# Wd of every expert kept on chip and addressed by a register, in a mixture-of-experts layer whose weights come by gather

## The chip, the cores and the metric

The kernel runs on one core of a Trainium2 chip. The metric is the device time of one execution in microseconds; where several executions were made, the median is given. The engines are named as the profile names them: PE (matrix multiply, with PEld for its weight loads), DVE (vector), ACT (scalar), POOL (the general engine, which here also issues the indirect DMAs) and SP (which issues the plain DMAs). All data are 32-bit floats.

## The reference, cut to what matters

Eight sequences of 256 tokens with 128 features pass through four blocks, each with a layer norm in front and a residual behind: a gated delta-net attention of 16 heads, a small feed-forward with the signs of a weight matrix, a causal softmax attention (16 query heads in 4 groups), and a mixture of experts. The change touches only the last. What it computes, for a token `x` and its normalised form `n`:

```python
s = softmax(n @ Wr.T)                    # 8 experts
s1, s2, e1, e2 = top2(s)                 # two largest and their experts
y = 0
for s_i, e in ((s1, e1), (s2, e2)):
    h = relu(n @ Wg[e].T) * (n @ Wu[e].T)    # 512 hidden features
    y += s_i / (s1 + s2 + eps) * (h @ Wd[e].T)
out = x + y
```

Each expert has three matrices of 512 x 128 (`Wg`, `Wu`) and 128 x 512 (`Wd`), 262 KB each; all eight experts' `Wd` are 2.1 MB.

## The kernel before, in words

The kernel has two stages. The first, up to about 883 us of the span, is the gated delta-net attention; its result `xr` is stored to DRAM (`x1`) sequence by sequence at line 953. The second stage opens new pools at line 995, loads `x1` back into eight tiles `x0` to `x7` (line 1003) and the weights of the later blocks (lines 1005 to 1019) with SP, and does the other three blocks.

Nothing in the second stage is scheduled by the compiler's order. Each part of the work is a Python generator that yields `Unit`s: the engine, an estimated duration, what it needs, which buffers it takes and gives back, what it sets, and how much later a DMA's data land (`lands`). The function `merge` plans all generators against each other on this estimate and emits the instructions in the planned order. An engine executes its instructions in this order, and waits on semaphores for what comes from other engines.

The experts work on token lists. Sequences 0 to 5 form one segment (12 token tiles of 128) and sequences 6 and 7 a second (4 token tiles). For each segment `lists_of` makes, on DVE and PE, a list of slots sorted by expert, padded so that every slot tile of 128 rows belongs to one expert: 31 slot tiles for the first segment and 15 for the second, 46 in all. It leaves `seg.tok` (which token stands in each slot), `seg.at` (where a token's two slots are) and `seg.ex`. In the kernel before, `seg.ex` (the tile `exi`) holds for slot tile k, in partition p, the row number 128 x expert + p.

Then for every slot tile k:

- `fetched()` (line 1463, POOL) gathers `we`, the tile of weights of the slot tile's expert, by an indirect DMA of 128 rows of 6144 bytes (786 KB): per partition 512 elements each of `Wg`, `Wu` and `Wd`. There are 7 such buffers (`WE`).
- `gathered()` (line 1451, POOL) gathers `xs`, the 128 normalised token rows (64 KB), into one of 8 buffers.
- `turned_rows()` (line 1474, PE) transposes them, and `taken_rows()` (line 1480, ACT) copies the result to SBUF as `xsT`.
- `hidden()` (line 1489, PE) makes 8 matmuls of 128 x 128 x 128 into the PSUM tile `gu`: four for `Wg`, four for `Wu`. There are two such PSUM tiles.
- `gated()` has ACT take the relu of the first half (line 1495) and DVE multiply it with the second (line 1497), which gives `h`.
- `projected_hidden()` (line 1504, PE) makes 4 accumulating matmuls with the `Wd` part of `we`, which gives `o`, and gives the buffer of `we` back.
- `stored()` copies `o` to `y` (line 1516, DVE) and stores it to DRAM (SP).

On PE the steady order is `o` of tile k, the transpose of tile k+4, `gu` of tile k+2. At the end `results()` gathers each token's two rows back (POOL) and `combined()` adds them, weighted, into `x` (line 1540, DVE) and stores the output.

A matmul in the profile is written `out<-stationary,moving`; the multiplication in 32-bit floats shows as two records for each `mm` call, so `gu` has 16 per tile and `o` 8.

Of the kernel before, what the change touches and what calls it, by code (L numbers as in the profile page):

```python
# [10 lines left out]
F32 = mybir.dt.float32  # L11
I32 = mybir.dt.int32
# [6 lines left out]
P = 128  # L19
B, T, D = 8, 256, 128  # L20
# [9 lines left out]
E, DFF = 8, 512  # L30
NF = DFF // P
# [4 lines left out]
WE = 7  # L36
# [110 lines left out]
def block_kernel(ctx: ExitStack, tc: tile.TileContext, a, out):  # L147
    nc = tc.nc
# [85 lines left out]
    wp = gx.enter_context(tc.tile_pool(name="g_w", bufs=1))  # L234
# [9 lines left out]
    with tc.tile_pool(name="g_ln", bufs=2) as lp, tc.tile_pool(name="g_lp", bufs=4, space=PSUM) as pp:  # L244
        x = lp.tile([P, NT, D], F32, name="x", bufs=1)
# [4 lines left out]
        for q in range(4):  # L250
# [3 lines left out]
            ps = pp.tile([P, 4, P], F32, tag="ps", name=f"lnpsa{q}")  # L254
# [5 lines left out]
        ps = pp.tile([P, NBC, 2 * NPR], F32, tag="ps", name="gateps")  # L260
# [33 lines left out]
        for lhsT, dst, name in ((le, pin, "pin"), (gt, dec, "dec"), (cross, pend, "pend")):  # L294
            ps = pp.tile(shape, F32, tag="ps", name=f"{name}ps")
# [3 lines left out]
    with (  # L299
# [36 lines left out]
        class Seq:  # L336


            def __init__(self):
                self.w, self.wv, self.sq = [], [], {}  # L340
                self.kq, self.vt, self.S = [None] * NH, {}, [None] * NH
                self.dm, self.pbs, self.at, self.g, self.gp = {}, {}, {}, {}, {}
                self.kk, self.ws, self.o, self.taken, self.oT, self.osq = {}, {}, {}, {}, {}, {}
                self.kb, self.kd, self.yn = {}, {}, {}
# [650 lines left out]
    with (  # L995
# [21 lines left out]
        nc.sync.dma_start(rank, a["rank"])  # L1017
        lc = wp.tile([P, N_LISTS], F32, name="lc")
        nc.sync.dma_start(lc, a["lists"])

        sgn = wp.tile([P, D], F32, name="sgn")
        neg = wp.tile([P, D], F32, name="neg")
# [39 lines left out]
        at = [Attended() for _ in range(B)]  # L1062
# [209 lines left out]
        class Tokens:  # L1272


            def __init__(self, t0, n):
                self.t0, self.n, self.s = t0, n, t0
                self.kt = (2 * n * P + E * (P - 1)) // P
                self.xn = dram.tile([n * P, D], F32, name=f"xn{t0}")
                self.ys = dram.tile([self.kt * P, D], F32, name=f"ys{t0}")
                self.lg = wp.tile([P, n, E], F32, name=f"lg{t0}")  # L1280
                self.xs, self.xsT, self.ps, self.h, self.o, self.y, self.we = {}, {}, {}, {}, {}, {}, {}

        segs, t0 = [], 0
        for n in LISTS:
# [17 lines left out]
        def lists_of(seg):  # L1302


            s, n, kt = seg.s, seg.n, seg.kt

            def tmp(name, shape, dtype=F32):
                return wp.tile([P] + shape, dtype, name=f"l_{name}{s}")
# [41 lines left out]
            ps = pp.tile([P, n + 1, E], F32, tag="ps", name=f"place{s}")  # L1350
# [50 lines left out]
            ex = tmp("ex", [kt])  # L1401
            nc.vector.tensor_reduce(ex, past, AX.X, ALU.add)
            nc.vector.tensor_scalar(ex, ex, float(E - 1), None, ALU.min)

            nc.vector.tensor_scalar(ex, ex, float(P), lc[:, L_ID : L_ID + 1], ALU.mult, ALU.add)
            seg.ex = tmp("exi", [kt], I32)
            nc.vector.tensor_copy(seg.ex, ex)
            yield Unit("DVE", 0.05, sets=(("experts", s),))

            intile = tmp("intile", [2, n, kt])  # L1410
# [9 lines left out]
            for c0 in range(0, 2 * n, step):  # L1420
# [6 lines left out]
                if c0 == 0:  # L1427
                    ps = pp.tile([P, kt], F32, tag="ps", name=f"token{s}")
# [29 lines left out]
        def fetched():  # L1458

            for seg, k in every:  # L1460
                yield Unit("POOL", 1.25, needs=(("experts", seg.s),), take=("we",), sets=(("we", seg.s, k),), lands=5.0)
                seg.we[k] = sp.tile([P, 3, NF, P], F32, tag="we", name=f"we{seg.s}_{k}", bufs=WE)
                nc.gpsimd.indirect_dma_start(
                    out=seg.we[k].rearrange("p a f c -> p (a f c)"),
                    out_offset=None,
                    in_=a["we"],
                    in_offset=bass.IndirectOffsetOnAxis(ap=seg.ex[:, k : k + 1], axis=0),
                )

        def turned_rows():  # L1470
# [11 lines left out]
        def hidden():  # L1482

            for seg, k in every:
                yield Unit("PE", 1.75, needs=(("x", seg.s, k, 0), ("we", seg.s, k)), take=("p2",), give=("xsT",), sets=(("gu", seg.s, k),), late=0.3)
                seg.ps[k] = p2.tile([P, 2, NF, P], F32, tag="p2", name=f"gu{seg.s}_{k}")
                for i in range(2):
                    for f in range(NF):
                        mm(seg.ps[k][:, i, f], seg.we[k][:, i, f], seg.xsT[k], start=True, stop=True)  # L1489
# [8 lines left out]

        def projected_hidden():
            for seg, k in every:  # L1500
                yield Unit("PE", 0.88, needs=(("h", seg.s, k),), take=("ps",), give=("h", "we"), sets=(("o", seg.s, k),), late=0.2)
                seg.o[k] = pp.tile([P, D], F32, tag="ps", name=f"o{seg.s}_{k}")
                for f in range(NF):
                    mm(  # L1504
                        seg.o[k],
                        seg.h[k][:, f],
                        seg.we[k][:, 2, f],
                        start=(f == 0),
                        stop=(f == NF - 1),
                    )  # L1510
# [34 lines left out]
        with tc.manual_schedule():  # L1545
            merge(
                [
                    turned_rows(),
                    taken_rows(),
                    stored(),  # L1550
                    projected_hidden(),
                    contexts(),
                    routes(),
                    layers(),
                    gathered(),
                    fetched(),
                    masked(),
                    exponentials(),
                    taken_exps(0),
                    scores(),  # L1560
                    gated(),
                    *[lists_of(seg) for seg in segs],
                    turned_exps(),
                    results(),
                    taken_exps(1),
                    combined(),
                    hidden(),
                ],
                dict(
                    ps=4, p2=2, qkv=2, scs=SCS, aT=16, den=4, xs=XS, xsT=3, h=4, y=4, yg=8, we=WE,  # L1570
                ),
                slack=0.1,
            )
# [76 lines left out]
```

## Time and profile before

| | before |
|---|---|
| median of three runs | 1315.72 us (1313.47 to 1318.91) |
| the profiled execution | 1320.55 us, with a span of 1318.80 |
| first stage (delta-net) | 0 to about 883 us |
| opening of the second stage | 883 to 907 us |
| second attention, and lists | 907 to 1133 us |
| expert tiles | 1133 to 1302 us |
| last gathers, sums and stores | 1302 to 1318.8 us |
| PE, DVE, ACT, POOL busy in the whole span | 82%, 70%, 57%, 44% |
| gathers' queue (software) | 41.30 MB of 95.38 MB moved |

The profile is of one execution, and its span is a little shorter than the execution's time. The stages have different limits, so the shares of the whole span say little about one of them. In the lines below, a table by stage gives for each stretch of time its length, the busy time of each engine with the number of instructions in brackets, the granted clock of PE as a share of full speed, the share of time in which the 16 DMA engines were busy, and the rate. A line of a group gives line, engine, operation, tiles and shapes, then the busy time and the mean duration in ns of one, and after the second bar the idle time of the engine ahead of these instructions with what ended it. A line of the timeline gives start, length, engine and instruction; SPq is SP's issue of a DMA, and PEldq stands for PE's sequencer in front of a weight load.

### The profile page before, as it was taken

To read this page: it belongs to the slowest core of one execution; us is meant where nothing else is said; L and a number is where in the kernel's file an instruction comes from. 1 tells how busy PE (TensorE), PEld (TensorE's weight loads), DVE (VectorE), ACT (ScalarE), POOL (GpSimd) and SP (SyncE) were. 2 spreads that over 40 slices of the span, in tenths; PEclk is the share of its full clock that TensorE was granted. 3 is DMA by queue.
4 is the path that set the end of the run, shared out by engine and by line. 5 is a ranking of instruction groups with operands and counts; after the bars stand their busy time and mean duration, and the time that the engine had idled before them with its cause. 6 is when DMAs were issued, how large, how long until landed. Compare 5 with 4: busy or idle time off the path is not lost.

```text
span 1318.8 us, 37752 instructions
## 1 busy us (share of the span) xinstructions
PE 1082.3 (82%) x15052; PEld 851.4 (65%) x15052; DVE 925.9 (70%) x2930; ACT 746.8 (57%) x1847; POOL 580.1 (44%) x1067
## 2 busy tenths in 40 slices
PE   3778688889898899898898986965788888889964
PEld 3345477577677677676676775853555555889963
DVE  4378957978878798788888686445777879452323
ACT  3457467577576577667676573444677776322211
POOL 1127628328247128418338146002322332566664
PEclk9779899899899899999899897786898887899997
DMA  3113320230321130230220122010000003388962
GB/s 113 44 33 74 85 59 20 59 79 18 78 63 38 26 102 19 58 87 22 70 71 24 47 67 49 4 41 20 5 6 5 6 9 118 132 263 279 304 221 75
DMA packets 120752, 95.38 MB, mean 72 GB/s; under 512 B 75296, under 2 KB 109344, under 8 KB 120448
## 3 DMA queue, kind: packets, MB, share of 16 engines
q1 hardware_dynamic: 110848, 51.18, 14.8%
q0 software_dynamic: 9120, 41.30, 9.5%
q8 instruction: 119, 1.95, 0.6%
q10 hardware_dynamic: 608, 0.48, 0.1%
q14 instruction: 57, 0.47, 0.1%
HBM read 77.20 MB, written 15.60 MB: 70 GB/s over the span
## 4 chain that ended last, share of the span: by engine, by line
PE 44%; DVE 32%; ACT 13%; issue 5%; POOL 4%; another core or an unknown queue 1%; DMA 1%; SPq 1%; POOLq 0%; DVEq 0%; ACTq 0%
DVE y L383 7%; PE gu L1489 6%; DVE yv L383 5%; PE W L708 4%; PE o L1504 3%; PE O L708 3%; ACT vt L907 3%; PE yps L943 2%; PE projv L375 2%; PE kk L561 2%; PE proj L375 2%; PE oTps L919 2%; PE pb L528 1%; PE av L1242 1%; PE X L665 1%
## 5 line engine op out<-in xcount | busy, mean ns | idle before, releaser
L383 DVE SCALAR_TENSOR_TENSOR y<-proj,conv,y 128x255 f32<-128x255 f32 (+2 forms) x384 | 154.1, 472 | 34.5 <-ACT y L378 34.4
L383 DVE SCALAR_TENSOR_TENSOR yv<-projv,conv,yv 128x255 f32<-128x255 f32 (+2 forms) x384 | 154.7, 471 | 29.3 <-ACT yv L378 29.0
L636 POOL TENSOR_TENSOR md<-md,tmp 128x31 f32<-128x31 f32 (+15 forms) x248 | 134.3, 542 | 19.4
L630 POOL TENSOR_TENSOR tmp<-md,nb 128x31 f32<-128x31 f32 (+15 forms) x248 | 126.4, 510 | 19.1
L1179 ACT ACTIVATE scs<-scs,low 128x128 f32<-128x128 f32 (+1 forms) x256 | 113.5, 447 | 22.8 <-DVE low L1150 22.4
L907 ACT ACTIVATE vt<-vt,rs 128x128 f32<-128x128 f32 x256 | 77.9, 390 | 39.5 <-DVE rs L322 39.5
L516 POOL TENSOR_TENSOR rla<-cst,la 128x512 f32<-128x512 f32 x32 | 33.4, 1042 | 145.2 <-PE pb L528 96.4
L1489 PE MATMUL gu<-xsT,we 128*128 128x128 f32 x736 | 95.2, 284 | 1.1 <-issue 0.7
L1489 PEld LDWEIGHTS gu<-xsT,we 128*128 128x128 f32 x736 | 91.1, 201 | 1.7 <-issue 1.0
L375 PE MATMUL proj<-xT,w 128*128 128x256 f32 x256 | 75.5, 422 | 17.6 <-DVE yv L383 7.0
L375 PE MATMUL projv<-xT,wv 128*128 128x256 f32 x256 | 77.0, 429 | 14.2 <-ACT y L378 4.3
L561 PE MATMUL kk<-kq 64*64 64x128 f32 x1024 | 76.3, 289 | 14.7 <-ACT kq L392 12.8
L561 PEld LDWEIGHTS kk<-kq 64*64 64x64 f32 x1024 | 59.0, 141 | 37.9 <-issue 20.4
L1150 DVE CUSTOM_DVE_ANT_0 scs<-sc,cst 128x128 f32<-128x128 f32 (+1 forms) x256 | 75.9, 349 | 9.9 <-PE sc L1120 9.9
L1516 DVE COPY y<-o 128x128 f32<-128x128 f32 x46 | 13.4, 291 | 95.9 <-PE xsT L1474 32.4
L1495 ACT ACTIVATE h<-gu 128x512 f32<-128x512 f32 x46 | 27.5, 598 | 93.6 <-PE xsT L1474 39.0
L708 PE MATMUL O<-ws,at 64*64 64x128 f32 x1024 | 69.5, 279 | 11.1 <-ACT mark L798 5.7
L1199 PE MATMUL tp<-cst,scs 128*128 128x128 f32 x384 | 74.6, 318 | 4.6 <-ACT scs L1179 3.7
L547 POOL TENSOR_TENSOR dm<-dm,cst 128x512 f32<-128x512 f32 x32 | 40.6, 1271 | 85.6 <-ACT dm L537 85.5
L708 PE MATMUL W<-vt,mt 64*64 64x128 f32 x1024 | 77.0, 284 | 0.7 <-ACT yn L802 0.4
L1199 PEld LDWEIGHTS tp<-cst,scs 128*128 128x128 f32 x384 | 52.8, 163 | 32.3 <-ACT scs L1179 29.7
L590 POOL TENSOR_TENSOR kq<-kq,pbs 128x256 f32<-128x256 f32 x48 | 34.4, 727 | 87.4 <-issue 36.1
(274 smaller groups left out, 2973.6 us busy)
## 6 DMA issues: line engine op xcount, KB each, us to landing
w<-in_wqkv SPq DMA_DIRECT2D x64, 128.0 KB
wv<-in_wqkv SPq DMA_DIRECT2D x64, 128.0 KB
md<-in_eye SPq DMA_DIRECT2D x8, 512.0 KB
raw<-nlt SPq DMA_DIRECT2D x32, 128.0 KB
nb<-raw SPq DMA_DIRECT2D x8, 512.0 KB
inv<-md SPq DMA_DIRECT2D x8, 512.0 KB
mt<-inv SPq DMA_DIRECT2D x32, 128.0 KB
ys<-y SPq DMA_DIRECT2D x46, 64.0 KB
```

Of the source, the lines that this page charges most:

```text
L375: mm(ps[:, j, :], w()[:, j, :], xT, start=True, stop=True)
L383: nc.vector.scalar_tensor_tensor(y[:, j, s:], ps[:, j, : T - s], conv[:, i, KW - 1 - s : KW - s], y[:, j, s:], ALU.mult, ALU.add)
L547: nc.gpsimd.tensor_tensor(q.dm[c], q.dm[c], le64.unsqueeze(1).to_broadcast([P, NPR, C]), ALU.mult)
L561: mm(ps[rows(h), i], k[:, 0, cols], k[:, :, cols], start=True, stop=True)
L630: nc.gpsimd.tensor_tensor(to, md[:, :n, s : s + 1].to_broadcast([P, n, m]), nb[:, s : s + 1, s + 1 :].to_broadcast([P, n, m]), ALU.mult,)
L636: nc.gpsimd.tensor_tensor(md[:, :n, s + 1 :], md[:, :n, s + 1 :], to, ALU.add)
L708: ins[which].append(mm(*args[:3], start=args[3], stop=args[4]))
L907: nc.scalar.activation(o[:, i], o[:, i], AF.Copy, scale=rs[:, c, h : h + 1])
L1150: q.last[p] = nc.vector.tensor_tensor_reduce(sc[:, m], q.pss[p][g // 2][:, g % 2, m], mask, -(HD**-0.5), -NEG, ALU.add, ALU.min, q.low[p][ ...
L1179: nc.scalar.activation(sc[:, m], sc[:, m], AF.Exp, bias=q.low[p][:, g, m : m + 1], scale=-1.0, accum_out=q.den[j][:, g, m0 + m : m0 + m + 1],)
L1199: nc.tensor.transpose(q.tp[p, g][:, k, m, :], q.sc[p, g][:, m, k * P : (k + 1) * P], ident)
L1489: mm(seg.ps[k][:, i, f], seg.we[k][:, i, f], seg.xsT[k], start=True, stop=True)
```

## The change

All experts' `Wd` is loaded once, by one plain DMA of SP at the start of the second stage, into a tile `wd` of 16 KB in every partition. The gather of a tile brings only `Wg` and `Wu` (rows of 4096 bytes, 524 KB), into a smaller buffer (28 instead of 42 KB in every partition for all seven). `seg.ex` now holds the bare expert number, and a new list `seg.wrows` the row numbers for the gather. `hidden()` loads the expert number of its tile into a register of PE, and gives the buffer of `we` back; `projected_hidden()` reads its moving operand from `wd` at an offset that it computes from this register. The planner's estimate of when a gather has landed goes from 5.0 to 4.0 us. On the host the arrays are put in the new order.

```diff
@@ 1017
         lc = wp.tile([P, N_LISTS], F32, name="lc")
         nc.sync.dma_start(lc, a["lists"])
+        wd = wp.tile([P, E * DFF], F32, name="wd")
+        nc.sync.dma_start(wd, a["wd"])
@@ 1401
             nc.vector.tensor_scalar(ex, ex, float(E - 1), None, ALU.min)
-
-            nc.vector.tensor_scalar(ex, ex, float(P), lc[:, L_ID : L_ID + 1], ALU.mult, ALU.add)
             seg.ex = tmp("exi", [kt], I32)
             nc.vector.tensor_copy(seg.ex, ex)
+
+            nc.vector.tensor_scalar(ex, ex, float(P), lc[:, L_ID : L_ID + 1], ALU.mult, ALU.add)
+            seg.wrows = tmp("wrows", [kt], I32)
+            nc.vector.tensor_copy(seg.wrows, ex)
@@ 1458
-                yield Unit("POOL", 1.25, needs=(("experts", seg.s),), take=("we",), sets=(("we", seg.s, k),), lands=5.0)
-                seg.we[k] = sp.tile([P, 3, NF, P], F32, tag="we", name=f"we{seg.s}_{k}", bufs=WE)
+                yield Unit("POOL", 1.25, needs=(("experts", seg.s),), take=("we",), sets=(("we", seg.s, k),), lands=4.0)
+                seg.we[k] = sp.tile([P, 2, NF, P], F32, tag="we", name=f"we{seg.s}_{k}", bufs=WE)
                 nc.gpsimd.indirect_dma_start(
...
-                    in_offset=bass.IndirectOffsetOnAxis(ap=seg.ex[:, k : k + 1], axis=0),
+                    in_offset=bass.IndirectOffsetOnAxis(ap=seg.wrows[:, k : k + 1], axis=0),
@@ 1482
-                yield Unit("PE", 1.75, needs=(("x", seg.s, k, 0), ("we", seg.s, k)), take=("p2",), give=("xsT",), sets=(("gu", seg.s, k),), late=0.3)
+                yield Unit("PE", 1.75, needs=(("x", seg.s, k, 0), ("we", seg.s, k)), take=("p2",), give=("xsT", "we"), sets=(("gu", seg.s, k),), late=0.3)
+                seg.ev[k] = nc.values_load(
+                    seg.ex[0:1, k : k + 1],
+                    engines=[mybir.EngineType.PE],
+                    min_val=0,
+                    max_val=E - 1,
+                    skip_runtime_bounds_check_because="at most E - 1 by the minimum that was taken",
+                )
@@ 1498
-                yield Unit("PE", 0.88, needs=(("h", seg.s, k),), take=("ps",), give=("h", "we"), sets=(("o", seg.s, k),), late=0.2)
+                yield Unit("PE", 0.88, needs=(("h", seg.s, k),), take=("ps",), give=("h",), sets=(("o", seg.s, k),), late=0.2)
...
-                        seg.we[k][:, 2, f],
+                        wd[:, bass.ds(seg.ev[k] * DFF + f * D, D)],
```

In the built program the multiplication and addition for the address become four register instructions on PE per slot tile, one ahead of each `o` matmul, and the load of the number one more. The order of the other instructions on PE and on ACT is the same as before. On SP the load of `x0` (line 1003) stands behind the last store of the first stage (line 953) instead of ahead of it, and waits for it.

More of the change, by code (lines that the diff above doesn't have):

```diff
@@ L1280, in __init__ @@
                 self.lg = wp.tile([P, n, E], F32, name=f"lg{t0}")
-                self.xs, self.xsT, self.ps, self.h, self.o, self.y, self.we = {}, {}, {}, {}, {}, {}, {}
+                self.xs, self.xsT, self.ps, self.h, self.o, self.y, self.we, self.ev = {}, {}, {}, {}, {}, {}, {}, {}
         segs, t0 = [], 0
@@ L1627 @@
         "rank": np.tile(np.arange(E, 0, -1, dtype=np.float32), (P, 1)),
-        "we": np.concatenate(
-            [
-                t(i["L1_ffn_Wg"]),
-                t(i["L1_ffn_Wu"]),
-                t(i["L1_ffn_Wd"]).reshape(E, NF, P, D).transpose(0, 2, 1, 3).reshape(E, P, NF * D),
-            ],
-            axis=2,
-        ).reshape(E * P, 3 * DFF),
+        "we": np.concatenate([t(i["L1_ffn_Wg"]), t(i["L1_ffn_Wu"])], axis=2).reshape(E * P, 2 * DFF),
+        "wd": t(i["L1_ffn_Wd"]).reshape(E, NF, P, D).transpose(2, 0, 1, 3).reshape(P, E * DFF),
     }
```

## The prediction

> **What bounds the kernel now.** I read the table by stage first, because the busy shares of the whole span (PE 82%, DVE 70%) mix stages with different limits. The change acts from 883 us on, and mostly in the expert tiles, which run from 1132.7 to 1301.1 us. Columns: stretch, length, busy time (and instructions) of the five engines, granted TensorE clock, DMA share, GB/s.
>
> ```profile
> core 0: us, PE busy (x) PEld busy (x) DVE busy (x) ACT busy (x) POOL busy (x), PEclk, DMA share, GB/s
> 883.00:907.00 24.00, 7.07 (x20) 4.73 (x18) 6.31 (x24) 1.74 (x4) 5.85 (x25) 0.57 0.29 81
> 1133.00:1302.00 169.00, 147.67 (x1247) 142.11 (x1246) 59.25 (x172) 37.83 (x94) 101.03 (x118) 0.95 0.71 229
> 1190.00:1210.00 20.00, 19.72 (x175) 19.35 (x174) 6.21 (x13) 5.71 (x14) 12.21 (x13) 1.00 0.85 270
> 1230.00:1250.00 20.00, 18.93 (x163) 18.17 (x162) 6.31 (x14) 5.82 (x15) 12.66 (x14) 1.00 0.92 309
> 1270.00:1290.00 20.00, 12.51 (x88) 12.32 (x89) 5.13 (x15) 3.18 (x8) 11.87 (x14) 0.83 0.47 147
> ```
>
> Where the DMA engines are fullest (0.92, 309 GB/s), PE is busy for 18.93 of 20 us. The stretch that PE loses time in (12.51 of 20) has a half-empty DMA. So I asked who waits for a weight gather. In the groups (busy, mean ns, then idle time before them and its releasers) the answer is nobody:
>
> ```profile
> L1489 PE MATMUL gu<-xsT,we 128*128 128x128 f32 x736 | 95.2, 284 | 1.1 <-issue 0.7 <-ACT xsT L1480 0.4
> L1463 POOL DMA_INDIRECT we<-in_we,l_exi x46 | 44.3, 964 | 56.4 <-PE xsT L1474 25.7 <-DVE low L1150 18.9 <-issue 4.4
> ```
>
> `gu`, the reader of the gathered weights, idles 1.1 us in 46 tiles, none of it for a DMA. It is the gather that waits for PE, to get a buffer back: the gather of tile 20 was issued at 1193.1, had landed by 1197.65 and was read at 1207.52. The weights lie ready some 10 us early. The tiles are bound by PE. One period of two tiles, by the timeline (start, length, engine, line):
>
> ```profile
> 1213.98 0.68 DVE L1497 TENSOR_TENSOR h<-gu,h 128x512 f32<-128x512 f32 x1
> ...
> 1215.47 1.06 PE L1504 MATMUL o<-we,h 128*128 128x128 f32 x8
> 1216.36 0.27 PE L1474 MATMUL xsT<-cst,xs 128*128 128x128 f32 x1
> 1216.47 1.95 PE L1489 MATMUL gu<-xsT,we 128*128 128x128 f32 x16
> ...
> 1217.97 0.69 DVE L1497 TENSOR_TENSOR h<-gu,h 128x512 f32<-128x512 f32 x1 [0.24 <-ACT h L1495]
> ...
> 1218.71 1.16 PE L1504 MATMUL o<-we,h 128*128 128x128 f32 x8 [0.29 <-issue]
> ...
> 1219.82 1.95 PE L1489 MATMUL gu<-xsT,we 128*128 128x128 f32 x16
> ```
>
> The first tile takes 2.79 us (gu 1.79, o 0.89, xsT 0.11). Its `h` was ready at 1214.66, 0.81 us before PE began `o` at 1215.47: a led tile. In the next one `h` comes at 1218.66 and `o` starts at 1218.71: no lead, and 3.35 us. From tile 16 to 34 every second tile is like that. Over all 46 the median is 3.03 us; 46 x 2.79 = 128.3 us would be the floor.
>
> Beyond that PE is held up by a few long stalls, in which the profile finds no local releaser:
>
> ```profile
> DVE y L1516 <- remote: 11.5, 2, 9.5
> ACT h L1495 <- remote: 10.0, 2, 6.0
> ```
> ```profile
> 1272.90 9.50 another core or an unknown queue
> 1283.34 2.08 PE o L1504 x8
> ```
>
> A stall is followed by half-clock matmuls (2.08 us for an `o` of 0.89). I put the long stalls at 11.4 us, the slow clock behind them at 5, and the late `h` of every second tile at 7: 23 us in all. Such waits occur only after 1080 us, where the gathers run.
>
> **The change part by part**, against the profiled execution, 1320.55 us (span 1318.80 and 1.75 around it), which is 4.83 over the median of 1315.72; the differences are then put on the median.
>
> *Bytes.* Each gather brings 524 KB instead of 786: 12.1 of 36.2 MB go, and 2.1 MB come once. The Trainium skill, "DMA: Bandwidth & Descriptors", gives a transfer as about 2 us and its bytes at 436 GB/s; that would be 3.80 us a gather before and 3.20 after, a gain of 46 x 0.60 = 27.6 us if gathers set the pace. The row of the gathers says they do not. Directly: 0. If the lead of 10 us were gone, a slower gather would show as `gu` waiting for a DMA.
>
> *Load of wd* (2.1 MB): SP's next issue after it is the store of `xn`, which waits over 40 us anyway; at the 309 GB/s seen it takes 6.8 us, in a stretch with a DMA share of 0.29; its first reader is the first `o`, at 1142.8. Cost 0; its cover is 240 us.
>
> *SP's order.* The schedule of the changed kernel puts the load of x0 (L1003) behind the last store of stage one (L953) and makes it wait for that store's landing. Before:
>
> ```profile
> 883.29 0.34 SPq L1003 DMA_DIRECT2D x<-x  x1
> 883.72 0.38 SPq L953 DMA_DIRECT2D x<-xr  x1
> 884.15 3.32 SPq L1003 DMA_DIRECT2D x<-x  x7
> 886.44 0.29 DVE L195 BATCH_NORM_STATS2 stf<-x 128x6 f32<-128x128 f32 x1 [2.90 <-DMA x<-x]
> ```
>
> The store can go at 883.6 (its data are there at 883.54) and lands about 2.3 us later, so x0 is issued at 886.0 instead of 883.29: +2.7. Queued behind it on SP are seven loads of x and the eight of weights, +2.0 each. DVE's `stf` waits for x0, POOL's Newton steps for `stf`, and PE for both; nothing else is there to do (PE is busy 7 of 24 us). On the path: +2.7.
>
> *DVE.* Two more converts (0.18 us by the row of the one there is), both in the list chain that the first gather and the tokens wait for: +0.4, 0 to 0.4.
>
> *Gathers' order on POOL.* Each `we` gather now waits for the end of gu(k-7) instead of o(k-7), and the `xs` of a later tile is queued behind it. The tightest is xs of tile 5, at about 1138.2 instead of 1134.5, needed at 1146.7; a 64 KB gather lands in some 3 us. 0, with about 4 us of margin. ACT's order does not change.
>
> *Registers on PE.* Per tile one load of the expert's number ahead of `gu`, and four register operations, one ahead of each `o` matmul. The trace of before has neither. The nearest row on PE is its event instruction:
>
> ```profile
> L1474 PEldq EVENT_SEMAPHORE  x20: 51/51/51, 1200.3 to 1259.0; - x20
> ```
>
> Register operation: 0.05 by that row as the lower end, 0.20 (four such, as each combines three or four operations) as the upper; I take 0.10. Load: 0.05 as the lower end. The nearest work that reads a few words and hands them on is a step of POOL's 128x2 chain (0.28 from start to start); PE's event is three times as long as the 17 ns of other engines, so 3 x 0.28 = 0.85, which I take. Here a rule speaks against the change: the Trainium skill, "Runtime: NRT & Kernel Launch", has register loads at about 1.3 us where they come from HBM; this one reads SBUF, and no run here shows it. Upper end 1.3. A matmul with a register address: 0 to 0.06 more, take 0.03.
>
> These instructions lie in PE's stream between "h is there" and "gu may go". What they may take unseen is the time the array works on `o` and xsT, 1.00 us (1215.47 to 1216.47), and in a led tile the lead as well (0.81, up to 1.2 in the early tiles). They take 4 x 0.10 + 0.85 + 0.12, and two events with 0.15: 1.52. In led tiles that fits (1.81). In the about 23 without a lead `gu` comes 0.52 late: 23 x 0.52 = 12.0 us. With 0.05 everywhere: 0. With 1.3 and 0.20: 1.4 to 1.5 late, 33. DVE, ACT and the buffers only follow PE here.
>
> *Relief.* If the late signals come from the DMA load, a third less of it takes part of the 11.4 us of stalls away. Bounds 0 and 23; the heaviest stretch (0.92) has no such stall and the one of 9.5 us stands at 0.47, so I take a quarter, -3; a stall that goes exposes the late `h` next.
>
> Sum: 2.7 + 0.4 + 12.0 - 3 = +12.1, so 1332.7 in that profile's terms and 1327.8 on the median.
>
> **The rivals.**
> 1. *The control is hidden* (loads near 0.2 us). Then 2.7 + 0.4 - 1 = +2: 1318. For it: PE's events pass behind pending work in 51 ns. Against it: every second tile has no lead at all.
> 2. *The late signals go* (faster). One mechanism: the releases that PE's end sends to ACT and DVE are held up while gathers fill the DMA engines, from 1132 to 1287. Price up to 23 us; with 3.1 of losses and up to 6 of control, -14 to -20: about 1301. It decides once the relief is over 3.1 + 6.6 and the control. For it: these waits occur only in this stage, and a third of the bytes go. Against it: they do not follow the DMA share.
> 3. *The load stops PE.* If it isn't executed while the array works but takes its time after `o`, 1 to 2 us in each of 46 tiles: +46 to +92, 1365 to 1410. For it: the value has to return before the first register operation. Against it: `gu` follows it and needs no register.
> 4. That the bytes don't go is excluded: the gather's rows are 4096 B instead of 6144.
>
> **How the numbers follow.** Late `gu`: 0.50, 1328, its own range 1317 to 1349 (load from 0.3 to 1.3). Hidden: 0.20. Relief: 0.20. Stop: 0.10. About 0.5% (6.6 us) is what a measurement can tell from no change. The first case is slower with 0.43 and the same with 0.07; the second the same with 0.14, else split; the third faster with 0.17; the fourth slower. Faster 0.20, same 0.23, slower 0.57. The range, 1303 to 1360, leaves out half of the relief and nearly all of the stop.
>
> **What would show it.** In the profile after: x0 issued near 886.0 and `stf` near 889.1; `gu` waiting for nothing by DMA, as before; loads and register operations on PE near 0.85 and 0.10 us; a gap of about half a microsecond between xsT and `gu` in tiles without a lead; the group of gathers waiting for `gu`. The prediction is wrong if the gap is absent (case 1), if the 9.5 us wait and the late `h` are gone (case 2), or if the gap is in every tile (case 3).

## The result, and the profile after

| | before | after |
|---|---|---|
| median | 1316.73 us (1313.30 to 1320.02) | 1324.13 us (1319.08 to 1325.95) |
| ratio | 1 | 1.0056, 95% interval 1.0040 to 1.0073 |
| profiled execution, span | 1320.55, 1318.80 us | 1324.21, 1322.43 us |

The changed kernel is 7.4 us slower. In the two profiles the span differs by 3.6 us only, since that of before was a long one. By stages (from the starts of the instructions that bound them):

| stage | before | after |
|---|---|---|
| to the last `xr` of the delta-net | 883.2 | 884.5 |
| opening, last `xr` to first scores `scs` | 25.15 | 28.24 |
| second attention and lists, to the first `gu` | 224.3 | 224.8 |
| expert tiles, first `gu` to last `o` | 168.3 | 167.2 |
| tail | 17.7 | 17.7 |

The first stage, which the change doesn't touch, differs by 1.2 us already, so a difference of one or two us between two profiles means little. The opening's +3.1 is the one that stands out. The table by stage of the changed kernel, columns as before:

```profile
core 0: us, PE busy (x) PEld busy (x) DVE busy (x) ACT busy (x) POOL busy (x), PEclk, DMA share, GB/s
883.00:912.00 29.00, 10.08 (x52) 6.46 (x47) 6.21 (x24) 3.20 (x5) 5.77 (x25) 0.57 0.41 139
1190.00:1210.00 20.00, 17.78 (x156) 17.30 (x155) 5.12 (x14) 4.64 (x12) 12.10 (x14) 1.00 0.63 184
1230.00:1250.00 20.00, 19.53 (x172) 19.04 (x170) 5.92 (x14) 5.22 (x13) 12.49 (x15) 1.00 0.73 219
1270.00:1290.00 20.00, 13.95 (x105) 12.61 (x104) 5.14 (x13) 3.65 (x9) 11.81 (x13) 0.90 0.46 132
```

The DMA share in the tiles fell from 0.85 and 0.92 to 0.63 and 0.73, and PE is no better filled for it: 17.78 and 19.53 us of 20 instead of 19.72 and 18.93. The groups of `gu` and of the gathers:

```profile
L1501 PE MATMUL gu<-xsT,we 128*128 128x128 f32 x736 | 95.0, 282 | 3.6 <-issue 3.3 <-ACT xsT L1485 0.4
L1468 POOL DMA_INDIRECT we<-in_we,l_wrows x46 | 44.3, 963 | 50.3 <-DVE low L1153 19.1 <-PE xsT L1479 18.4 <-issue 8.0
```

`gu` waits for no DMA, as before, and the late signals of PE are still there. A measure of them is the time from the end of the last record of a tile's `gu` to the start of ACT's relu, 0.04 us where nothing is late. It is over 0.5 us in 21 of the 46 tiles before and in 26 after, and adds up over all tiles to 55 and 54 us. Here is one such tile of before, whose `gu` ends at 1215.63:

```profile
1213.68 1.95 PE L1489 MATMUL gu<-xsT,we 128*128 128x128 f32 x16
1217.34 0.60 ACT L1495 ACTIVATE h<-gu 128x512 f32<-128x512 f32 x1 [3.19 <-PE xsT L1474]
```

In the trace the semaphore events of this `gu`, of the `o` behind it and of the xsT after that stand together, at 1217.32, 1217.41 and 1217.44. PE has been in the next `gu` since 1216.47, and the relu starts 0.02 us after the first of the three. So the signal is late, and not the matmuls. The opening, by the timeline:

```profile
884.48 0.29 DVE L951 TENSOR_TENSOR xr<-yps,xr 128x128 f32<-128x128 f32 x1 [2.05 <-PE yps L943]
884.80 0.34 SPq L953 DMA_DIRECT2D x<-xr  x1
886.76 3.65 SPq L1003 DMA_DIRECT2D x<-x  x8
889.52 0.29 DVE L195 BATCH_NORM_STATS2 stf<-x 128x6 f32<-128x128 f32 x1 [4.75 <-DMA x<-x]
```

x0 is issued 1.96 us after the store, once this has landed, and `stf` starts 5.04 us after `xr` instead of 3.19. PE's pause before its first transpose grows from 8.88 to 10.64 us. Behind it come the score matmuls `sc`, first before, then after:

```profile
907.23 1.14 PE L1120 MATMUL sc<-kT,qT 32*128 32x512 f32 x8 [0.68 <-ACT kT L1093]
```
```profile
910.59 2.09 PE L1123 MATMUL sc<-kT,qT 32*128 32x512 f32 x8 [0.68 <-ACT kT L1096]
```

The granted clock in them was 1.00 before and 0.50 after. That is most of how +1.85 became +3.1 in this profile; in the three other profiles below with x0 behind the store (e2, e3, e9) `sc` took 1.14 us.

The register instructions, in the rows of their lines (ns: minimum, median, maximum):

```profile
L1491 PEldq TENSOR_LOAD <-l_exi x46: 295/302/491, 1136.3 to 1298.9; - x46
L1516 PEldq FUSED_REGOPS  x184: 51/55/60, 1144.7 to 1304.1; - x184
```

The load takes 0.30 us, not 0.85; the register operation 0.055, not 0.10. A tile without a lead, after:

```profile
1216.81 1.16 PE L1516 MATMUL o<-wd,h 128*128 x8 [0.22 <-issue]
1217.80 0.27 PE L1479 MATMUL xsT<-cst,xs 128*128 128x128 f32 x1
1217.91 1.96 PE L1501 MATMUL gu<-xsT,we 128*128 128x128 f32 x16
```

From `o` to `gu` it is 1.10 us; the same step before was 1.11 (1218.71 to 1219.82). It is 1.10 in most tiles without a lead, before, after, and in the run below that has no registers (e2). In the trace one of the four register operations of this tile has run ahead, at 1215.35, while the array was still on the `gu` in front. The second starts with `o` at 1216.81, and the event ahead of `gu` ends at 1217.79, 0.98 later: it just fits under the 1.10 that the array needs for `o` and xsT.

### The profile page after: what moved, and what is told of

The parts are those of the page before. It is cut to its first block, busy times and chain, and to the rows that moved or that the text cites. A ratio compares the mean times of both kernels' runs of the same rounds, so it can differ in the third digit from the quotient of the medians.

```text
span 1322.4 us, 37989 instructions
## 1 busy us (share of the span) xinstructions
PE 1086.4 (82%) x15052; PEld 853.1 (65%) x15052; DVE 925.8 (70%) x2932; ACT 746.9 (56%) x1847; POOL 580.6 (44%) x1067
## 4 chain that ended last, share of the span: by engine, by line
PE 43%; DVE 32%; ACT 13%; issue 6%; POOL 4%; DMA 1%; another core or an unknown queue 0%; POOLq 0%; SPq 0%; DVEq 0%; ACTq 0%
DVE y L383 7%; PE gu L1501 5%; DVE yv L383 5%; PE W L708 4%; PE o L1516 3%; PE O L708 3%; ACT vt L907 3%; PE projv L375 2%; PE kk L561 2%; PE yps L943 2%; PE proj L375 2%; PE pb L528 2%; PE vps L498 1%; PE X L665 1%; PE oTps L919 1%
## 5 line engine op out<-in xcount | busy, mean ns | idle before, releaser
L378 ACT ACTIVATE y<-proj,conv 128x256 f32<-128x256 f32 x128 | 55.6, 471 | 30.6 <-PE proj L375 30.2
```

Source lines behind the costliest of these rows:

```text
L378: nc.scalar.activation(y[:, j, :], ps[:, j, :], AF.Copy, scale=conv[:, i, KW - 1 : KW])
```

## The experiments

The kernels ran on several chips, each beside the kernel before on its own chip, which is what a ratio refers to. The chips are of two kinds: on some the kernel before takes 1317 to 1320 us, like the chip of the prediction, on others 1289. Below, "late" chips and "other" chips. The runs e1 to e12 were made on four chips, each in one session only, so that the chip and the time of the session can't be told apart.

| kernel | before on that chip | ratio and 95% interval |
|---|---|---|
| changed kernel | 1316.7 (late) | 1.0056 (1.0040 to 1.0073) |
| e1 own pool for wd | 1320.1 (late) | 1.0037 (1.0020 to 1.0054) |
| e2 no registers | 1320.1 (late) | 1.0059 (1.0042 to 1.0076) |
| e3 full rows | 1320.1 (late) | 1.0050 (1.0035 to 1.0065) |
| e4 before again | 1320.1 (late) | 1.0001 (0.9977 to 1.0025) |
| e5 plan of before | 1288.8 (other) | 1.0003 (0.9987 to 1.0020) |
| e6 row register | 1288.8 (other) | 0.9995 (0.9976 to 1.0014) |
| e7 wd unused | 1288.8 (other) | 1.0001 (0.9985 to 1.0017) |
| e8 no gather | 1288.8 (other) | 0.9992 (0.9974 to 1.0010) |
| e9 changed kernel | 1289.5 (other) | 0.9994 (0.9978 to 1.0010) |
| e10 combined | 1289.5 (other) | 0.9990 (0.9976 to 1.0005) |
| e11 combined | 1317.0 (late) | 1.0066 (1.0042 to 1.0090) |
| e12 no gather | 1317.0 (late) | 0.9933 (0.9903 to 0.9964) |

**e1: wd in a pool of its own.**

```diff
-        tc.tile_pool(name="t_w", bufs=1) as wp,
+        tc.tile_pool(name="t_w", bufs=1) as wp, tc.tile_pool(name="t_d", bufs=1) as dwp,
...
-        wd = wp.tile([P, E * DFF], F32, name="wd")
+        wd = dwp.tile([P, E * DFF], F32, name="wd")
```

> wd gets a pool of its own behind the pool of the weights; nothing else differs, and SP issues x0 ahead of the last store again, as in the kernel before. Theory 1 (the loss lies in the opening): the profiles show stf 5.04 us after the last xr instead of 3.19 (+1.85), and the first scores at half clock behind the longer pause of PE (k and sc +1.3); so 3.2 us of the 7.4 come back: about 1321, ratio to before 1.0033, and stf again 3.2 us after xr. Theory 2 (the loss lies in the tiles, by the registers): the opening's 3 us are hidden or made up later, 1323 to 1324. Theory 3 (all of the loss is the opening and what follows from it): 1317.

The timeline of e1:

```profile
886.56 0.29 DVE L951 TENSOR_TENSOR xr<-yps,xr 128x128 f32<-128x128 f32 x1 [2.05 <-PE yps L943]
886.60 0.34 SPq L1003 DMA_DIRECT2D x<-x  x1
...
889.63 0.29 DVE L195 BATCH_NORM_STATS2 stf<-x 128x6 f32<-128x128 f32 x1 [2.78 <-DMA x<-x]
```

x0 is issued ahead of the store, and `stf` is 3.07 us behind `xr` again. So it was wd in the pool `t_w` that put x0 behind the store. The likely reason, which was not taken apart, is that x0, as the first tile of `t_w`, waits for the last users of the whole pool's memory, and that wd stretched the pool over memory with later users. Over all profiles the split is clean: the four kernels with x0 behind the store (changed, e2, e3, e9) have their first scores 27.5 to 28.2 us after `xr`, all ten others 25.1 to 25.6. The cost of that step is thus 1.9 to 3.1 us, and 2.3 in most. In the total the ratio fell by 0.0019, 2.5 us, which would agree; but the two were measured apart, the intervals overlap, and e11, whose x0 is early too, has 1.0066. So it is the profiles that show this step, not the totals. 0.0037 (4.9 us) is left on this chip, so theory 3 falls.

**e2: no registers.** `values_load` is left out and `o` reads `wd[:, f * D : (f + 1) * D]`.

> The changed kernel without the load of the expert's number and the address registers: o always reads Wd of expert 0, so the choice of Wd is left out. The work of every engine is otherwise the same. Theory 1 (registers are hidden beside o, 0.93 us against 1.00 of cover): 1324, ratio to the changed kernel within 0.1%. Theory 2 (the registers cost what the prediction had, 12 us): 1312. Should the register-addressed matmuls hold up others, between these.

1.0059 against 1.0056: the 12 us don't come back. With the rows above, the registers are hidden.

**e3: full rows.** The gather and its buffer have three parts again, and the third is not read.

```diff
-                seg.we[k] = sp.tile([P, 2, NF, P], F32, tag="we", name=f"we{seg.s}_{k}", bufs=WE)
+                seg.we[k] = sp.tile([P, 3, NF, P], F32, tag="we", name=f"we{seg.s}_{k}", bufs=WE)
```

> The changed kernel, but its gathers bring 6144 bytes a row as before; the Wd part is not read. Order and instruction counts on every engine are those of the changed kernel. Theory of relief (late signals come from the bytes on the DMA engines): 3 to 10 us more than the changed kernel, 1327 to 1334. Rival (bytes don't matter, the number of gathers does): 1324, within 0.1%, and as many late h as in the changed kernel, but spread as before (every second tile).

1.0050: 12 MB more through the DMA engines don't cost the 3 us and more that a relief by bytes would have to be worth. The relief of the prediction is not there. Nor are the signals later with the bytes back: the relu is over 0.5 us late in 19 tiles, against 26 in the changed kernel.

**e4: before again.**

> The kernel before once more, for a second profile: how far its stages vary from one execution to the next. The first profile had 1320.55 us, 3.8 above the median of eight runs. Expected: 1313 to 1320, the opening (xr to stf 3.19 us) the same to 0.1 us, and the difference in the long stalls of the expert tiles.

The opening is 25.14 us (25.15 in the first profile), the tiles 168.5 (168.3), but attention and lists 227.4 against 224.3. The stalls were not what varies: the tiles agree in length, and the lateness of the relu adds up to 54 us against 55. A stage of one profile can be 3 us off, and the first stage, the same in all kernels, ends anywhere from 875 to 887 us, so small differences of stages can't be read from single profiles. Beside this profile, on the same chip, the tiles of all three changed forms are longer: 171.4 in e1, 173.8 in e2 and 170.1 in e3.

**e5 to e8**, each on top of e1, but for e7.

e5 has the planner's numbers of before, so that POOL, DVE, ACT and SP have the order of before:

```diff
-  ... take=("we",), sets=(("we", seg.s, k),), lands=4.0)
+  ... take=("we",), sets=(("we", seg.s, k),), lands=5.0)
...
-  ... give=("xsT", "we"), sets=(("gu", seg.s, k),) ...
+  ... give=("xsT",), sets=(("gu", seg.s, k),) ...
...
-  ... give=("h",), sets=(("o", seg.s, k),) ...
+  ... give=("h", "we"), sets=(("o", seg.s, k),) ...
```

> wd in its own pool, and the planner told as in the kernel before: the buffer of we comes back after o, a gather lands after 5.0. POOL, DVE, ACT and SP then have the order of the kernel before; bytes, registers and the two converts are those of the change. Own pool alone has left a loss of 0.37%, about 5 us. Theory A (the moved gathers cost the rest, by xs gathers queued behind we gathers that wait): ratio 1.000 to 1.001. Theory B (the rest is the converts, the load of wd or the registers' side effects): 1.003 to 1.004, no change against own pool.

e6 loads the register from the row numbers (`seg.wrows[0:1, k : k + 1]`, offset `seg.ev[k] * (DFF // P) + f * D`), and the converts for `exi` are left out:

> wd in its own pool, and the register is loaded from the gather's row numbers (partition 0 holds 128 times the expert), so that both extra converts on DVE go; nothing else differs from own pool. By the sum of the prediction 0.4 us, ratio 1.0034. If the converts push the list chain into a worse place (theory B), up to 2 us, 1.002.

e7 is the kernel before with the load of wd added, into a pool of its own and unused:

> The kernel before, and wd loaded into a pool of its own at the same place in SP's order, but never read: gathers and o as before. Only the load's 2.1 MB and the place of the other tiles differ. Prediction: hidden, ratio 1.000. If the load or the addresses are what is left of the loss: 1.003 to 1.004.

e8 has no weight gathers; `gu` reads one resident tile that is loaded at the start:

```diff
+        wgu = dwp.tile([P, 2, NF, P], F32, name="wgu")
+        nc.sync.dma_start(wgu.rearrange("p a f c -> p (a f c)"), a["we"][:P])
...
-                        mm(seg.ps[k][:, i, f], seg.we[k][:, i, f], seg.xsT[k], start=True, stop=True)
+                        mm(seg.ps[k][:, i, f], wgu[:, i, f], seg.xsT[k], start=True, stop=True)
```

> wd in its own pool, and no weight gathers: gu of every tile reads one resident copy of the Wg and Wu of expert 0 (the choice of these is left out). POOL has 46 indirect DMAs fewer, the DMA engines 24 MB less; PE's work is the same. Theory of relief by gathers (late signals to ACT and DVE and the long stalls come from the weight gathers): the stage of 168 us falls towards 46 x 2.79 = 128 and its filling, 145 to 150, so about 1300. Rival (they come from something else): 1320 to 1325, long stalls as before.

All four are within 0.1% of before, but before itself is 31 us shorter on this chip, so they don't tell what e1's rest comes from. They show something else. The table by stage of e7, which gathers as the kernel before:

```profile
1190.00:1210.00 20.00, 20.00 (x182) 20.00 (x181) 6.21 (x14) 6.52 (x15) 13.67 (x15) 1.00 0.98 324
1210.00:1230.00 20.00, 20.00 (x182) 20.00 (x181) 6.30 (x15) 6.13 (x15) 13.21 (x15) 1.00 1.00 331
```

The same gathers, a DMA share of 0.98 and 1.00, and PE is busy without a gap. The tiles take 137.4 us with full gathers (e7), 135.3 and 136.1 with light ones (e5, e6) and 135.3 with none (e8); the tail has 18.8, 20.1, 18.3 and 20.1. The 30 us of stalls and late `h` of the first profile do not exist on this chip, whatever is gathered: in none of the four does a relu start more than 0.36 us after its `gu`.

**e9 and e10: changed kernel and combined kernel, other chip.** e10 is e1 with the edits of e5 and e6.

> The changed kernel once more, beside the kernel before on the same chip. The last four ran on a chip where the kernel before takes 1288.8 us and a profile shows the expert tiles at 135 to 137 us instead of 168, with gathers and without. What the change costs in the opening (x0 behind the store: 2.3 to 3.1 us from the last xr to the first scores) must show on either kind of chip: ratio 1.0018 to 1.0025 where the tiles run at 2.79 us each. Where they run at 3.0 or more with late signals, 1.0056 as measured. Rival (the whole loss of 7.4 us is the kernel's own): 1.0056 on both.

> wd in its own pool, the register from the row numbers (no extra converts), and the planner told as in the kernel before, so that all engines' orders are those of the kernel before. What is left of the change: 12 MB fewer bytes, the registers and the load of wd. Expected: 1.000, within 0.1%, on both kinds of chip; faster than before only if the bytes count: below 0.998.

Here the changed kernel is as fast as before (0.9994), and so the loss of 7.4 us is no property of the kernel alone. In the profile the opening costs what it did (`stf` 5.34 us after `xr`, scores after 27.65), but the total doesn't show it: the 1.0018 that was expected lies above the interval. The tiles with the tail take 154.9 us against 156.2 in e7, which is less than a single profile can tell, so what makes up for the opening is not shown. The tiles of e9, by the timeline:

```profile
1206.53 1.95 PE L1501 MATMUL gu<-xsT,we 128*128 128x128 f32 x16
1208.32 1.06 PE L1516 MATMUL o<-wd,h 128*128 x8
1209.21 0.27 PE L1479 MATMUL xsT<-cst,xs 128*128 128x128 f32 x1
1209.32 1.95 PE L1501 MATMUL gu<-xsT,we 128*128 128x128 f32 x16
```

2.79 us from `gu` to `gu`, with all five register instructions in it, and 1.00 from `o` to `gu`. The relu of the first of these two `gu`, which ends at 1208.48, follows at once:

```profile
1208.52 0.60 ACT L1507 ACTIVATE h<-gu 128x512 f32<-128x512 f32 x1 [1.52 <-PE gu L1501]
```

**e11 and e12: combined and no gather, late chip.**

> The combined kernel (wd in its own pool, no extra converts, the orders of the kernel before) once more, in the hope of a chip where the tiles run at 3.0 us with late signals; the kernel before shows which (1315 to 1320 us there, 1289 on the other kind). There own pool alone had 1.0037. If what was left came from the moved gathers and the converts: 1.000. If it comes from the registers or the lighter gathers where signals come late: 1.003 to 1.004. On the other kind: 0.999 again.

> No weight gathers (gu reads one resident Wg and Wu of expert 0; wd in its own pool), beside the run above. On a chip with late signals: if the gathers make them late, the tiles fall from 168 to some 136 us, 1288 and a ratio of 0.976; if the chip makes them late whatever the kernel does, 165 to 170 us and 0.995 to 1.003. On the other kind of chip: 0.999 again, which leaves this open.

e11 settles that neither x0's place nor the converts nor the planner's order is what was left of the loss on late chips: without all three it is 1.0066, no less than the changed kernel's. e12 lies between its two theories. Its table by stage, and below it that of e11:

```profile
1139.00:1163.00 24.00, 23.02 (x196) 22.84 (x196) 9.22 (x31) 7.08 (x19) 10.40 (x21) 0.96 0.17 44
1185.00:1237.00 52.00, 52.00 (x468) 52.00 (x467) 16.30 (x37) 16.00 (x37) 18.49 (x20) 1.00 0.22 49
1237.00:1260.00 23.00, 15.42 (x117) 15.04 (x116) 6.45 (x17) 3.65 (x10) 14.35 (x16) 0.86 0.32 68
```
```profile
1190.00:1210.00 20.00, 19.46 (x172) 19.08 (x171) 6.51 (x19) 5.09 (x13) 11.27 (x12) 1.00 0.64 191
1210.00:1230.00 20.00, 19.25 (x165) 18.66 (x166) 6.12 (x14) 5.47 (x14) 12.41 (x14) 1.00 0.74 211
```

Without weight gathers the late `h` of the middle is gone: 52.00 of 52 us busy, every relu 0.04 us after its `gu`. The long stalls near the start and from 1237 on, where POOL begins to gather results, remain at a DMA share of 0.32. The tiles take 156.9 us instead of 171.2, and the time falls from 1324.0 to 1306.7, 17.4 us; in these two profiles the tiles and the tail together give 11.8 of it, and the first stage, whose code is the same, differs by 7.3. Over all tiles the lateness of the relu falls from 54 us to 23. So on late chips more than half of the late signals go with the weight gathers; a third fewer bytes per gather changes nothing (e3 against the changed kernel), and on other chips neither does anything at all.

The number of gathers would fit: in the middle of e12 POOL issues one in about 2.8 us and nothing is late, while from 1236 to 1252 it issues 13 in 16 us. This was not tried alone, and it would leave open why the other chips show none of it.

## Why the prediction was right, and where it was not

- **PE bounds the tiles, and the bytes are worth nothing directly:** shown. `gu` waits for no DMA in either profile; the 27.6 us estimated by the rule of the Trainium skill ("DMA: Bandwidth & Descriptors", the section on the anatomy of one DMA) did not come, and e3 and e8 say the same from both sides. What e12 gains without weight gathers goes with earlier signals, for nobody waited for the data.
- **x0's move, +2.7:** right in kind, and in size 1.9 at `stf` and 1.9 to 3.1 at the first scores, most where `sc` ran at a granted clock of 0.50. The prediction had the landing of the store right to 0.3 us. It named the wait; that wd in this pool causes it, and that a second pool undoes it, e1 showed.
- **Two converts, +0.4:** not resolved; e6 and e11, without them, show no gain.
- **Registers, +12.0:** this is the term that failed. The load is 0.30 us and not 0.85, the operation 0.055 and not 0.10, no extra time shows in the matmuls, and the stretch from the start of `o` to the event ahead of `gu` is 0.98 us against 1.10 of cover. Three of the four register operations lie in it, not four. It costs nothing, in tiles with and without a lead: the gap of half a microsecond, whose absence the prediction named as the sign of case 1 (control hidden), is absent. The tiles without a lead were about as many as it took, 16 in the trace of before and 5 more with a lead under 0.5 us. The row of PE's events (51 ns), which was given as the lower end, was the right one to take for the register operation, and the 1.3 us that the Trainium skill ("Runtime: NRT & Kernel Launch", the section on the launch sequence) has for loads from HBM is four times what a load from SBUF takes here.
- **Relief, -3:** failed too. With a third fewer bytes the late signals stay, 55 us of them before and 54 after. The most that their going could bring was also put too low, at 23 us: on the other chips, without them, the tiles with full gathers take 31 us less (137.4 in e7).
- **The load of wd:** hidden on the other chips, shown by e7 (1.0001, interval 0.9985 to 1.0017); it was not tried on a late chip.

So the total came out near by luck. Most of the forecast loss was 12 us of registers, and these were nothing. The loss on the chip of the comparison is 2.3 to 3.1 us of opening, as predicted, and another 4 to 5 that no term of the prediction holds and that are there on late chips only. Rival 1 (control hidden) had the mechanism right; of its +2, the totals on the other chips show nothing.

What these last 4 to 5 us are stays open. Without the opening's step, e1 is still 4.9 us above before (1.0037) and e11 8.7 (1.0066), with intervals that overlap. In the profiles the expert tiles of the changed forms take 170.1 to 173.8 us on late chips (e1, e2, e3, e11) against 168.3 and 168.5 in the kernel before, yet the profile of the changed kernel has 167.2, and a stage varies by 3 us. Taking away the registers (e2) or giving back the bytes (e3), each with the opening's loss in it, did not remove them, and orders and converts are excluded by e11. What all the changed forms share, and what was not taken apart on a late chip, is that wd is loaded and the other tiles lie elsewhere in memory, that `o` reads its operand from the resident tile, and that a gather's buffer is free after `gu` instead of after `o`, so that its gather can start earlier. No version tried beats the kernel before on both kinds of chip.

## What to carry to other kernels

Before taking bytes off a transfer, look at who waits for it: here nobody did, and removing a third of the weight bytes moved nothing, while the resident tile, put into the pool of the next stage's first load, made that load 2 us later. A big tile that is needed late goes into a pool of its own. Register loads and address arithmetic on PE are cheap beside matmuls as long as they fit under the array's queued work: here 0.98 us of them under 1.00 to 1.10.

## What the hardware showed that was not expected

- A load of a register from SBUF on PE took 0.30 us (0.41 until the next instruction of its sequencer), a fused register operation 0.055 (one in 0.13 us, with its matmul's issue); both ran while the array worked on `o`.
- The same kernel takes 1289 us on some chips and 1317 to 1320 on others. Most of the difference lies in one stage: the stage of 168 us in which POOL gathers takes 135 to 137 there. Where it is long, PE's semaphore events came up to 10 us after the matmul, often several at once, and more than half of this lateness went away with the weight gathers (54 to 23 us in the relu's starts). A profile from one chip had made these look like part of the kernel.
- A DMA share of 1.00 (331 GB/s) beside a PE without a gap: in this stretch full DMA engines did not slow matmuls whose operands had landed.
